# Summing an attention unit's values over all chunks of keys in one open PSUM bank

## The chip, the cores and the metric

The kernel runs on one core of a Trainium2 chip. The core has TensorE (PE, with its weight loads shown as PEld), VectorE (DVE), ScalarE (ACT), GpSimd (POOL) and SyncE (SP), which here only issues DMAs. TensorE writes its results to PSUM; the kernel plans with eight banks of 512 fp32 columns by 128 partitions. The metric is the device time of one execution in microseconds.

## The reference

Two layers (L0, L1) work on x of 4 x 512 x 320. Each layer has self-attention, cross-attention to a context of 4 x 1601 x 192, and a gated feed-forward part, all with a layer norm ahead and a residual behind. There are 20 heads of 16.

```python
def _attn(x, ctx, wq, wk, wv, wo, bo, heads):
    q = (x @ wq).reshape(b, n, heads, dh).transpose(0, 2, 1, 3)
    k = (ctx @ wk).reshape(b, j, heads, dh).transpose(0, 2, 1, 3)
    v = (ctx @ wv).reshape(b, j, heads, dh).transpose(0, 2, 1, 3)
    sim = jnp.einsum('bhid,bhjd->bhij', q, k) * scale
    a = jax.nn.softmax(sim, axis=-1)
    out = jnp.einsum('bhij,bhjd->bhid', a, v)
    return out.transpose(0, 2, 1, 3).reshape(b, n, heads * dh) @ wo + bo

h1 = _ln(x, n1_g, n1_b);  x = _attn(h1, h1, q1, k1, v1, o1_w, o1_b, heads) + x
h2 = _ln(x, n2_g, n2_b);  x = _attn(h2, context, q2, k2, v2, o2_w, o2_b, heads) + x
h3 = _ln(x, n3_g, n3_b)
a, g = jnp.split(h3 @ ff_w1 + ff_b1, 2, axis=-1)
x = a * jax.nn.gelu(g, approximate=False) @ ff_w2 + ff_b2 + x
```

## The kernel before

**Units and chunks.** The work is cut into units: one kind of attention, one batch element, one group of four heads. A layer has 20 self units and 20 cross units, then four feed-forward units. An attention unit goes over its keys in chunks of 128: 4 chunks in a self unit (512 keys), 13 in a cross unit (1601 keys, the last chunk has 65). The four heads of a group lie on four blocks of 32 partitions, so that four matmuls of 32 rows can run beside each other.

**One chunk.** `main` (L1272) does for each chunk two rounds, one for heads 0 and 1 and one for heads 2 and 3. A round takes two score tiles `st` (128 keys x 512 queries, three matmuls each: two with the split queries, L1285, and one that subtracts the maximum, L1288) and, beside them, usually two tiles `sps` of the *next* unit (L1093), from which VectorE finds that unit's maxima over the keys (L1112; a rest tile in L1131). ScalarE takes the exponential of each `st` into a buffer in SBUF (L1298); `place()` (L249) hands out these buffers in a ring of 9 or 12. `round_of` (L1258) interleaves the matmuls of scores and maxima, so that one kind runs on partitions 0 to 63 while the other runs on 64 to 127; in the second round the scores of heads 2 and 3 begin before the maxima tiles. If the unit in hand is ahead of schedule with maxima, extra rounds of them alone are put in.

**The values.** `values(c)` (L1305) multiplies the exponentials of chunk c with the values: four heads fill the four blocks of 32 partitions of one bank `av` (eight matmul instructions in the trace, L1312). It is held back by one chunk (`late`, `flush`): it is issued behind the scores of chunk c+1, and the last chunk's values behind the first scores of the next unit. Each chunk's `av` is a result of its own. ScalarE copies the first into `u.o` (L1323); each later one goes by a ScalarE copy into a ring buffer (L1328) and a GpSimd addition onto `u.o` (L1329). In the last cross unit of a layer, marked `last`, VectorE copies and adds instead (L1323, L1325), and no maxima run beside the scores. After the last chunk `add_finish` (L1168) puts the store of `u.o`, and after a batch element's fifth group the division by the sums and the output projection (`ops`, L1225), on the list of other work.

**Other work and its order.** Projections of queries (`qps`, L876), keys (`kps`, L910 for self and L953 for the context, the latter four banks at a time, read by ScalarE and VectorE in L963) and values (`vps`, L1028, and L1046 for the context, four banks at a time, read in L1054), norms, transposes and output projections wait in queues with costs and due times. `steps` (L471) takes from them behind each chunk's values, by rounds and credits. The order of PE's instructions comes from these rounds and credits.

**Banks.** Which of the eight banks a tile gets is planned in Python when the program is written out. `Pace` (L54) books an estimated time for every matmul, exponential, copy and maximum; `bank` (L161) takes the bank with the earliest booked release (`first`, L66), and marks it as taken (`give`, L71) until an instruction of ScalarE or VectorE that reads it is booked (`see`, L81). On the chip the first matmul into a bank waits for the last reader of the bank's previous tile. PE has one queue: what stands behind a waiting matmul waits with it.

Of the kernel before, what the change touches and what calls it, by code (L numbers as in the profile page):

```python
# [13 lines left out]
ALU = mybir.AluOpType  # L14
# [39 lines left out]
class Pace:  # L54
# [16 lines left out]
    def give(self, i, t):  # L71
        self.bank_of = {n: k for n, k in self.bank_of.items() if k != i}
        self.bank_of[t.tensor.name] = i
        self.opens[i] = self.free[i]
        self.free[i] = 1e9
# [5 lines left out]
    def see(self, r):  # L81
        i = r.ins
        kind = type(i).__name__
        banks = {self.bank_of.get(x.bass_ap.tensor.name) for x in list(i.ins) + list(i.outs) if hasattr(x, "bass_ap")}
        banks.discard(None)
        sizes = []
        for x in list(i.outs) + list(i.ins):
            if hasattr(x, "bass_ap"):
                n = 1
                for _, k in list(x.ap)[1:]:  # L90
                    n *= k
                sizes.append(n)
        if kind == "InstMatmult":
            (b,) = banks
            mode = tuple(i.tile_size or (P, P))
            if mode != self.mode:
                self.at["PE"] = max([self.at["PE"], *self.tiles.values()]) + 0.25
                self.tiles, self.mode = {}, mode
            pos = tuple(i.tile_position or (0, 0))
            self.at["PE"] = max(self.at["PE"], self.opens.get(b, 0.0) + 0.1)  # L100
            one = i.ins[0].dtype == F32R
            cost = max(sizes[0] * (1 if one else 4) / 2280, 0.06)
            self.tiles[pos] = max(self.tiles.get(pos, 0.0), self.at["PE"]) + cost
            self.ready[b] = self.tiles[pos]
            return r
        eng = "ACT" if "Activat" in str(i.engine) else "DVE"
        n = max(sizes)
        cost, more, late = (0.112 + n / 1400, 0.16, 0.1) if eng == "ACT" else (0.065 + n / 960, 0.16, 0.17)
        if eng == "DVE" and not banks:
            cost = 0.13 + n / 5900 if "Transpose" in kind else 0.18 + n / 960  # L110
        start = max([self.at[eng]] + [self.ready[b] + late for b in banks])
        self.at[eng] = start + cost
        for b in banks:
            self.free[b] = start + cost + more
        return r
# [13 lines left out]
def kernel(ctx: ExitStack, tc: tile.TileContext, x, context, ws, out):  # L129
# [18 lines left out]
    nc = tc.nc  # L148
# [8 lines left out]
    ps = ctx.enter_context(tc.tile_pool(name="ps", bufs=1, space=PSUM))  # L157
    pace_of = Pace()
    see = pace_of.see

    def bank(name, shape=(P, 512)):  # L161
        i = pace_of.first()
        t = ps.tile(list(shape), F32, tag=f"bank{i}", name=name)
        pace_of.give(i, t)
        return t
# [83 lines left out]
    def place():  # L249
        these = places[at_place["kind"]]  # L250
        at_place["i"] = (at_place["i"] + 1) % len(these)
        return these[at_place["i"]]
# [158 lines left out]
    start = {"on": True}  # L411
# [31 lines left out]
    def run(chain):  # L443
        costs, _, ready, _, f = chains[chain].popleft()
        assert ready(), chain
        f()
        clock["credit"] -= sum(costs)
# [15 lines left out]
    def next_cost():  # L463
        name = pick()
        return None if name is None else sum(chains[name][0][0])

    def tick():
        clock["round"] += 1
        clock["credit"] = max(-2.0, min(4.0, clock["credit"] + pace()))
# [34 lines left out]
    def until(test, name):  # L504
        while not test():
            assert chains[name], name
            run(name)
# [638 lines left out]
    def max_reduce(u):  # L1146
        if u.pm is not None:
            see(nc.vector.tensor_reduce(
                u.nm.rearrange("p (j t) -> p t j", t=NQ), u.pm, AX.X, ALU.max, negate=True
            ))  # L1150
# [102 lines left out]
    def flush():  # L1253
        for f in late:
            f()
        late.clear()

    def round_of(scores, maxima, turn=False):  # L1258

        todo = [f() for f in scores] + [f() for f in maxima]  # L1260
        if len(todo) == 3 and turn and [len(p) for p, _ in todo] == [3, 3, 2]:
            for j, i in [(0, 0), (1, 0), (0, 1), (1, 1), (2, 0), (2, 1), (0, 2), (1, 2)]:
                todo[j][0][i]()
        else:
            for i in range(max((len(passes) for passes, _ in todo), default=0)):
                for passes, _ in todo:
                    if i < len(passes):
                        passes[i]()
        for _, then in todo:
            then()  # L1270

    def main(u, give, nxt):  # L1272

        pr = {}
        if at_place["kind"] != u.kind:
            at_place.update(kind=u.kind, i=min(at_place["i"], len(mine) - 1))

        def score(c, j):
            r = min(P, u.nkeys - c * P)
            rows = slice(j * SLOT, (j + 1) * SLOT)  # L1280
            st = bank("st")
            keys = u.kT[rows, u.k0 + u.cols[c] : u.k0 + u.cols[c] + r].bitcast(F32R)

            def product(e):
                see(nc.tensor.matmul(st[:r, :], lhsT=keys, rhs=u.q[rows, :, e].bitcast(F32R), start=(e == 0), stop=False))  # L1285

            def less_maximum():
                see(nc.tensor.matmul(  # L1288
                    st[:r, :],
                    lhsT=units_of[rows, :r].bitcast(F32R),  # L1290
                    rhs=u.mrow[rows, :].bitcast(F32R),
                    start=False,
                    stop=True,
                ))

            def exponential():
                p = place()
                see(nc.scalar.activation(p[:r], st[:r], AF.Exp))  # L1298
                pr[c, j] = p

            return [lambda: product(0), lambda: product(1), less_maximum], exponential

        last = nxt is None or nxt.kind == "ff"

        def values(c):  # L1305
            if u.g in (0, 2):
                until(lambda: units[u.i - u.g].vmade[u.g // 2] > c, "values")
            ps = bank("av")
            r = min(P, u.nkeys - c * P)
            for j in range(HG):  # L1310
                head = (c * H + u.g * HG + j) * VW
                see(nc.tensor.matmul(  # L1312
                    ps[j * SLOT : (j + 1) * SLOT, :],
                    lhsT=columns_of[:r, head : head + SLOT],
                    rhs=pr.pop((c, j))[:r, :],
                    start=True,
                    stop=True,
                ))
            u.valued = c + 1

            if c == 0:
                u.o = three.tile([P, N], F32, tag="o", name="o")
                see((nc.vector.tensor_copy if last else nc.scalar.copy)(u.o, ps))  # L1323
            elif last:
                see(nc.vector.tensor_tensor(u.o, ps, u.o, ALU.add))  # L1325
            else:
                vo = place()
                see(nc.scalar.copy(vo, ps))  # L1328
                nc.gpsimd.tensor_tensor(u.o, u.o, vo, ALU.add)  # L1329
            if u.valued == u.nch:  # L1330
                add_finish(u)

        for c in range(u.nch):
            extra = []
            if last:

                round_of([lambda j=j: score(c, j) for j in range(HG)], [])
                tick()
            else:
                for odd in range(2):  # L1340
                    if odd:
                        tick()
                    pair, rounds = give(2 * c + odd)
                    extra += rounds
                    round_of([lambda j=j: score(c, j) for j in ((2, 3) if odd else (0, 1))], pair, odd)
            u.scored = c + 1

            if extra:
                round_of([], extra[0])
            flush()  # L1350
            late.append(lambda c=c: values(c))
            steps(None, 1 if extra or c == u.nch - 1 else 3)
            for i, e in enumerate(extra[1:]):
                if i and next_cost() is not None:
                    run(pick())
                round_of([], e)
            if not last and c == u.nch - 3:
                max_reduce(nxt)
                max_end(nxt)
            if loads:  # L1360
                loads.popleft()()
# [300 lines left out]
```

## Time and profile before

| | |
|---|---|
| median of 3 runs | 2959.55 us (2958.13 to 2960.76) |
| profiled execution, first to last instruction | 2956.1 us |
| around it, to the median | 3.5 us |
| granted TensorE clock, mean | 0.998 |
| PE busy | 2905.4 us (98%) |
| VectorE busy | 2017.1 us (68%) |
| ScalarE busy | 1950.7 us (66%) |
| GpSimd busy | 1361.8 us (46%) |

The first layer's self-attention runs to about 370 us, its cross-attention to about 1190, its feed-forward part to about 1500; the second layer follows in the same order. In a row of a group, `av<-pr,vals` names the tile written and the tiles read, then come partitions and elements, the count, the busy time, the mean duration in ns of one, and the idle time before them with what ended it. Buffers of the ring carry several names (`pr`, `wself`, `w`, `w1r`), since the ring borrows room in weight tiles. In a row of waits stand the engine that waited, what it waited for, the total in us, how many times, and the longest. In a timeline stand the start and the duration in us, the engine, the line and what it does; a bracket gives the idle time of the engine before it and what ended that. A busy PE in this profile is not PE at its peak: matmuls overlap, and their ends are modelled.

### The profile page before, as it was taken

Reading aid. Unit: us, or ns where it says so; the run is one execution under the profiler, and the core shown is the slowest. Engines: PE = TensorE matmul, PEld = TensorE weight load, DVE = VectorE, ACT = ScalarE, POOL = GpSimd, SP = SyncE. Lnnn points to the kernel's source line nnn. Section 1 sums busy time; section 2 is a strip of 40 time slices with the busy share of each in tenths; the row PEclk is TensorE's granted clock in tenths of the full one; section 3 lists DMA queues with packets and bytes.
Section 4 is the critical chain, followed back from the end, with each engine's and each line's share of the span. In section 5 each row is a group of like instructions: output and inputs, shape, how many; then the busy total and the mean of one; then the engine's idle time right before and its main releaser. Section 6 shows DMA issues by size and latency. Waiting matters only on the chain.

```text
span 2956.1 us, 92200 instructions
## 1 busy us (share of the span) xinstructions
PE 2905.4 (98%) x37842; PEld 1608.3 (54%) x37842; DVE 2017.1 (68%) x3893; ACT 1950.7 (66%) x4029; POOL 1361.8 (46%) x1714
## 2 busy tenths in 40 slices
PE   9999999999999999999999999999999999999999
PEld 4555556555555555455554555655555555544555
DVE  7777887887888788322257778878878878872221
ACT  4867677887887888511147766778878888893111
POOL 4556455555555554312125664555555555541110
PEclk9999999999999999999999999999999999999999
DMA  4434222222122221300124332121221221212000
GB/s 117 120 102 116 68 71 55 55 71 70 32 71 64 48 56 28 113 6 0 33 53 112 95 95 74 50 69 34 60 70 36 58 69 43 52 52 57 12 11 12
DMA packets 221151, 178.01 MB, mean 60 GB/s; under 512 B 137652, under 2 KB 175416, under 8 KB 220728
## 3 DMA queue, kind: packets, MB, share of 16 engines
q1 hardware_dynamic: 219928, 171.05, 22.4%
q8 instruction: 297, 4.87, 0.7%
q10 hardware_dynamic: 800, 1.06, 0.1%
q14 instruction: 126, 1.03, 0.1%
HBM read 54.67 MB, written 29.56 MB: 28 GB/s over the span
## 4 chain that ended last, share of the span: by engine, by line
PE 88%; DVE 7%; ACT 2%; POOL 1%; issue 1%; DMA 1%; SPq 0%; ACTq 0%; POOLq 0%; DVEq 0%
PE av L1312 22%; PE st L1285 15%; PE sps L1093 11%; PE fps L1407 9%; PE yps L1462 6%; PE kps L953 4%; PE ops L1225 4%; DVE pm L1112 3%; PE st L1288 3%; PE qps L876 3%; PE vps L1046 3%; PE fps L1420 2%; DVE nmax L1112 2%; PE vps L1028 2%; PE kps L910 2%
## 5 line engine op out<-in xcount | busy, mean ns | idle before, releaser
L1112 DVE TENSOR_REDUCE pm<-sps 128x1 f32<-128x512 f32 x1920 | 1190.4, 681 | 100.3 <-PE sps L1093 93.8
L1093 PE MATMUL sps<-kT,q 32*128 32x512 f32 (+1 forms) x6400 | 1059.6, 401 | 10.3 <-DMA kT<-stage 3.5
L1298 ACT ACTIVATE pr<-st 128x512 f32<-128x512 f32 (+1 forms) x1710 | 905.0, 603 | 182.1 <-PE st L1288 170.3
L1285 PE MATMUL st<-q,kT 32*128 32x512 f32 (+1 forms) x5440 | 864.4, 423 | 2.1 <-ACT stage L918 1.2
L1329 POOL TENSOR_TENSOR o<-o,pr 128x512 f32<-128x512 f32 x359 | 460.2, 1282 | 583.0 <-ACT pr L1328 575.4
L1312 PE MATMUL av<-pr,vals 128*32 128x512 f32 (+1 forms) x3420 | 632.8, 605 | 21.0 <-DVE nmax L1112 2.8
L1285 PEld LDWEIGHTS st<-q,kT 32*128 32x128 f32 (+1 forms) x5440 | 461.9, 180 | 351.0 <-ACT pr L1298 133.8
L1093 PEld LDWEIGHTS sps<-kT,q 32*128 32x128 f32 x6400 | 554.8, 183 | 96.0 <-ACT pr L1298 11.6
L1288 PE MATMUL st<-m,units 32*128 32x512 f32 (+1 forms) x2720 | 550.5, 399 | 1.0 <-DMA m<-turned 0.9
L1298 ACT ACTIVATE wself<-st 128x512 f32<-128x512 f32 (+1 forms) x867 | 463.2, 604 | 79.7 <-PE st L1288 74.9
L1112 DVE TENSOR_REDUCE nmax<-sps 128x1 f32<-128x512 f32 x640 | 397.2, 682 | 112.6 <-PE sps L1093 111.1
L1329 POOL TENSOR_TENSOR o<-o,wself 128x512 f32<-128x512 f32 x191 | 244.8, 1282 | 287.9 <-ACT wself L1328 277.9
L1312 PE MATMUL av<-wself,vals 128*32 128x512 f32 (+1 forms) x1734 | 368.6, 605 | 8.1 <-ACT pr L1298 1.6
L1407 PE MATMUL fps<-hT,w 128*128 128x512 f32 x640 | 283.7, 596 | 0.0
L1430 ACT ACTIVATE pr<-fps,b 128x512 f32<-128x512 f32 x80 | 54.7, 687 | 346.0 <-PE fps L1420 245.4
L1288 PEld LDWEIGHTS st<-m,units 32*128 32x128 f32 (+1 forms) x2720 | 251.6, 180 | 20.0 <-POOL stage L765 1.1
L1328 ACT COPY pr<-av 128x512 f32<-128x512 f32 x359 | 220.6, 615 | 11.6 <-PE av L1312 11.2
L1407 PEld LDWEIGHTS fps<-hT,w 128*128 128x128 f32 x640 | 118.8, 190 | 149.4 <-issue 148.5
L1312 PEld LDWEIGHTS av<-pr,vals 128*32 128x32 f32 (+1 forms) x3420 | 91.2, 108 | 187.8 <-DVE pm L1112 83.3
L765 POOL TENSOR_SCALAR stage<-stage 128x256 fp32r<-128x256 f32 (+1 forms) x155 | 106.2, 685 | 158.6 <-ACT stage L918 82.9
L953 PEld LDWEIGHTS kps<-ctxT,w 32*128 32x128 f32 (+1 forms) x4992 | 112.6, 160 | 40.7 <-ACT pr L1298 17.8
L1225 PEld LDWEIGHTS ops<-wo,aT 112*32 112x32 f32 (+1 forms) x3072 | 98.6, 110 | 64.4 <-issue 39.6
(115 smaller groups left out, 3068.1 us busy)
## 6 DMA issues: line engine op xcount, KB each, us to landing
q<-stage SPq DMA_DIRECT2D x154, 256.0 KB
kT<-w SPq DMA_DIRECT2D x120, 208.0 KB
outs<-o SPq DMA_DIRECT2D x80, 256.0 KB
kT<-stage SPq DMA_DIRECT2D x76, 128.0 KB
aT<-outs SPq DMA_DIRECT2D x32, 224.0 KB
oturn<-over SPq DMA_DIRECT2D x32, 224.0 KB
kT<-w SPq DMA_DIRECT2D x40, 144.0 KB
w<-in_L_xattn_ff_w_dram SPq DMA_DIRECT2D x20, 256.0 KB
```

The costliest lines, as they stand in the source:

```text
L953: see(nc.tensor.matmul(ps[to : to + n, :PIECE], lhsT=wk_q[rows, k, u.g * GD : u.g * GD + n], rhs=first.kvT[rows, k, at : at + PIECE], star ...
L1093: see(nc.tensor.matmul(out, lhsT=u.q[rows, t // 2, e, t % 2 * P : (t % 2 + 1) * P].bitcast(F32R), rhs=u.kT[rows, keys].bitcast(F32R), star ...
L1112: see(nc.vector.tensor_reduce(to[:, j : j + 1], ps, AX.X, ALU.max, negate=(ns == 1)))
L1225: see(nc.tensor.matmul(ps[f : f + m, : D // 2], lhsT=aT[:n, k, t * P + f : t * P + f + m], rhs=wo[:n, k, cols], start=(k == 0), stop=(k == 2),
L1285: see(nc.tensor.matmul(st[:r, :], lhsT=keys, rhs=u.q[rows, :, e].bitcast(F32R), start=(e == 0), stop=False))
L1288: see(nc.tensor.matmul(st[:r, :], lhsT=units_of[rows, :r].bitcast(F32R), rhs=u.mrow[rows, :].bitcast(F32R), start=False, stop=True,))
L1298: see(nc.scalar.activation(p[:r], st[:r], AF.Exp))
L1312: see(nc.tensor.matmul(ps[j * SLOT : (j + 1) * SLOT, :], lhsT=columns_of[:r, head : head + SLOT], rhs=pr.pop((c, j))[:r, :], start=True, s ...
L1328: see(nc.scalar.copy(vo, ps))
L1329: nc.gpsimd.tensor_tensor(u.o, u.o, vo, ALU.add)
L1407: see(nc.tensor.matmul(ps, lhsT=w1[:, k, i * FF + c * P : i * FF + (c + 1) * P], rhs=u.hT[:, k, :], start=ahead and k == 0, stop=not ahead ...
L1462: see(nc.tensor.matmul(ps[:, :D], lhsT=hid[c][:, t * P : (t + 1) * P], rhs=w2[:, c, :], start=(c == 0), stop=(c == NHC - 1),))
```

## The change

A unit takes one bank for `av` when its first values are computed and keeps it until its last. The first chunk's matmuls start the sum, the others add to it, and one copy takes it to `u.o` after the last chunk (by ScalarE, in a `last` unit by VectorE). The copies and additions of the other chunks go: 3 of each in a self unit, 12 in a cross unit. The matmuls, their order and the due times stay.

```diff
         def values(c):
             if u.g in (0, 2):
                 until(lambda: units[u.i - u.g].vmade[u.g // 2] > c, "values")
-            ps = bank("av")
+            if c == 0:
+                u.av = bank("av")
+            ps = u.av
             r = min(P, u.nkeys - c * P)
             for j in range(HG):
                 head = (c * H + u.g * HG + j) * VW
...
                     rhs=pr.pop((c, j))[:r, :],
-                    start=True,
-                    stop=True,
+                    start=(c == 0),
+                    stop=(c == u.nch - 1),
                 ))
             u.valued = c + 1
 
-            if c == 0:
+            if u.valued == u.nch:
                 u.o = three.tile([P, N], F32, tag="o", name="o")
                 see((nc.vector.tensor_copy if last else nc.scalar.copy)(u.o, ps))
-            elif last:
-                see(nc.vector.tensor_tensor(u.o, ps, u.o, ALU.add))
-            else:
-                vo = place()
-                see(nc.scalar.copy(vo, ps))
-                nc.gpsimd.tensor_tensor(u.o, u.o, vo, ALU.add)
-            if u.valued == u.nch:
                 add_finish(u)
```

## The prediction

> **What bounds the kernel now.** I read the page's head and its chain of waits first, then the list of waits, then the timeline of a few chunks. The page:
>
> ```profile
> span 2956.1 us, 92200 instructions
> ...
> PE 2905.4 (98%) x37842; PEld 1608.3 (54%) x37842; DVE 2017.1 (68%) x3893; ACT 1950.7 (66%) x4029; POOL 1361.8 (46%) x1714
> ...
> PE 88%; DVE 7%; ACT 2%; POOL 1%; issue 1%; DMA 1%; SPq 0%; ACTq 0%; POOLq 0%; DVEq 0%
> ...
> L1298 ACT ACTIVATE pr<-st 128x512 f32<-128x512 f32 (+1 forms) x1710 | 905.0, 603 | 182.1 <-PE st L1288 170.3
> L1329 POOL TENSOR_TENSOR o<-o,pr 128x512 f32<-128x512 f32 x359 | 460.2, 1282 | 583.0 <-ACT pr L1328 575.4
> L1312 PE MATMUL av<-pr,vals 128*32 128x512 f32 (+1 forms) x3420 | 632.8, 605 | 21.0 <-DVE nmax L1112 2.8
> ...
> L1328 ACT COPY pr<-av 128x512 f32<-128x512 f32 x359 | 220.6, 615 | 11.6 <-PE av L1312 11.2
> ```
>
> TensorE is busy 98% of the span and carries 88% of the chain; ScalarE and GpSimd, from which the change takes work, carry 3% together. So what the change does to the time is decided by what it does to PE, and PE keeps every one of its matmuls. What can move is only when a PSUM bank is free for the next matmul. The list of waits says which banks PE's weight loads wait for:
>
> ```profile
> PEld av L1312 <- DVE pm L1112: 141.5, 328, 0.8
> ...
> PEld st L1285 <- ACT pr L1298: 133.8, 208, 0.8
> ...
> PEld av L1312 <- DVE nmax L1112: 59.0, 117, 1.4
> ...
> PEld av L1312 <- ACT pr L1298: 42.3, 98, 0.7
> ...
> PEld sps L1093 <- ACT pr L1298: 11.6, 33, 0.8
> ...
> PEld sps L1093 <- ACT pr L1328: 8.8, 54, 0.3
> ...
> PEld sps L1093 <- ACT wself L1328: 5.6, 35, 0.3
> ```
>
> The totals hold PE's change from one tile shape to the next, so they are no stalls by themselves. What counts is the names. The bank for `av` is most often one that VectorE has just released by a maximum (328 and 117 times), and 54 + 35 times a maximum tile `sps` waited for the copy out of `av`, which the change removes. The kernel runs at the edge of its eight banks. Two chunks of a cross-attention unit show how:
>
> ```profile
> 651.50 0.50 PE L1285 MATMUL st<-q,kT 32*128 32x512 f32 x2
> ...
> 651.51 0.65 PE L1093 MATMUL sps<-kT,q 32*128 32x512 f32 x2
> ...
> 651.96 0.62 ACT L1328 COPY wself<-av 128x512 f32<-128x512 f32 x1
> ...
> 652.31 0.48 PE L1093 MATMUL sps<-kT,q 32*128 32x512 f32 x1
> ...
> 652.63 0.18 PEld L1093 LDWEIGHTS sps<-kT,q 32*128 32x128 f32 x2 [0.16 <-ACT wself L1328]
> ...
> 653.29 1.07 PE L1312 MATMUL av<-pr,vals 128*32 128x512 f32 x8
> ...
> 654.28 0.50 PE L1285 MATMUL st<-q,kT 32*128 32x512 f32 x2
> ...
> 654.29 0.50 PE L1093 MATMUL sps<-kT,q 32*128 32x512 f32 x2
> ...
> 655.07 2.48 DVE L1112 TENSOR_REDUCE pm<-sps 128x1 f32<-128x512 f32 x4 [0.29 <-PE sps L1093]
> ...
> 655.16 0.54 PE L1093 MATMUL sps<-kT,q 32*128 32x512 f32 x2
> ...
> 655.34 2.06 ACT L1298 ACTIVATE pr<-st 128x512 f32<-128x512 f32 x4 [0.23 <-PE st L1288]
> ...
> 655.82 0.16 PEld L1312 LDWEIGHTS av<-wself,vals 128*32 128x32 f32 x8 [0.36 <-DVE pm L1112]
> 655.82 1.06 PE L1312 MATMUL av<-wself,vals 128*32 128x512 f32 x8
> ```
>
> The groups of maxima, by count, shortest/median/longest in ns, and first and last start:
>
> ```profile
> L1112 DVE TENSOR_REDUCE pm<-sps x1920: 623/681/694, 277.1 to 2637.7; 128x1 f32<-128x512 f32 x192
> L1112 DVE TENSOR_REDUCE nmax<-sps x640: 648/681/694, 20.0 to 1811.8; 128x1 f32<-128x512 f32 x160
> L1131 DVE TENSOR_REDUCE pm<-sps x160: 421/424/438, 362.0 to 2640.6; 128x4 f32<-128x264 f32 x160
> ```
>
> A chunk opens eight tiles in PSUM: two `st` and two `sps` at its start (654.28), two more `st` half a microsecond on, and the last `sps` (call it the eighth tile) at 655.16. The first of the eight to be released is a maximum: VectorE starts it at 655.07, it takes 0.68 (681 ns, below), so its bank is free at 655.75. At 655.16 all eight are therefore unread, and all eight banks are taken. `av` is the ninth tile: it starts at 655.82, when the first maximum ends. In the chunk at 651.50 the eighth tile had to wait instead until the copy out of the previous `av` (651.96 + 0.62) was done, and began at 652.63. So `av` borrows the eighth bank for a part of each chunk only.
>
> **The change part by part.**
>
> *The bank that stays open.* After the change `av` holds a bank from a unit's first values to its last, and seven are left for the eight tiles of a chunk. The order of PE's matmuls does not depend on the banks (they are laid out by rounds and credits), so the eighth tile must wait, in its old place, for a tile of its own chunk. In the second chunk that is the release that `av` waits for now: 655.82 instead of 655.16, 0.66 us late. PE's later matmuls stand behind it in order. From the eighth tile to `av` it is 0.66 us in both chunks (652.63 to 653.29, 655.16 to 655.82), and then `av` itself has nothing left to wait for; so `av` moves from 655.82 to 656.48 and the chunk grows by 0.66. In the first chunk the same release would come 1.54 after its start (655.82 - 654.28), at 653.04; the eighth tile now starts at 652.63, so it loses 0.41. The copy's lateness that this chunk pays today is thereby already given back.
>
> I take the two as equally frequent: the waits of `sps` for the copy are 89 of 680 chunks, but `st` and `sps` wait some 240 times more for exponentials of the chunk before (rows above), which makes the eighth tile late in the same way. Mean 0.535 us. Chunks: 40 self units of 4 and 40 cross units of 13 are 680. In the second chunk of each unit no values bank is open while the scores run (80 chunks), and the last cross unit of each layer has no maxima beside its scores (26, of which 2 are second chunks). That leaves 680 - 80 - 24 = 576, and 576 x 0.535 = **+308 us**. Lower end: 0.41 everywhere, +236. Upper end: the planner gives the eighth tile the bank of an `st`; the first exponential of the second chunk starts at 655.34 and takes 0.60 (603 ns in the page's row of L1298), so the release is at 655.94, 0.19 later: 576 x 0.725 = +418.
>
> *Chunks behind a group of four tiles.* The projections of keys and values from the context open four banks at once, and scores often follow at once:
>
> ```profile
> 805.69 2.23 PE L1046 MATMUL vps<-w,ctxT 32*128 32x192 f32 x48
> ...
> 807.61 0.54 PE L1285 MATMUL st<-q,kT 32*65 32x512 f32 x2
> ...
> 807.94 0.54 ACT L1054 COPY vals<-vps 128x192 f32<-128x192 f32 x2 [1.35 <-PE vps L1046]
> ...
> 807.98 0.62 DVE L1054 COPY vals<-vps 128x192 f32<-128x192 f32 x2 [1.51 <-PE vps L1046]
> ...
> 808.31 0.27 PEld L1285 LDWEIGHTS st<-q,kT 32*65 32x65 f32 x4 [0.19 <-ACT vals L1054]
> ```
>
> ```profile
> L1054 ACT COPY vals<-vps x96: 265/296/328, 324.4 to 2494.8; 128x128 f32<-128x128 f32 x48, 128x192 f32<-128x192 f32 x48
> ```
>
> ```profile
> L963 ACT COPY w<-kps x160: 245/248/254, 239.2 to 2577.9; 128x104 f32<-128x104 f32 x160
> ```
>
> At 807.61 four banks hold `vps`, four are free. With `av` open there are three, so the fourth tile waits for the first copy: 807.94 + 0.30 = 808.24, 0.63 late, and the wait for the eighth tile comes on top. There are 96/2 = 48 such groups of values and 160/2 = 80 of keys (half of each group's four copies are ScalarE's). Ends: nothing (hidden by another step in between) and 128 x 0.63 = +81. I take three quarters of the groups at 0.5 us, since the copies of `kps` are shorter: 96 x 0.5 = **+48 us**.
>
> *The copies and sums that go.* 40 x 3 + 40 x 12 less the 24 of the `last` units, again 576, chunks lose a ScalarE copy of 615 ns (354 us of ScalarE) and a GpSimd addition of 1282 ns (738 us); in the `last` unit of each layer 24 additions of VectorE go. On the path this is worth only the lateness counted above, since none of these engines carries the chain; PE's 98% of busy time is what hides it. If PE had slack, ScalarE would give at most its 2% of the chain, 59 us. ScalarE's queue gains: exponentials no longer stand behind a copy, but the first exponential of a chunk already waits for PE (655.34 above). GpSimd's other work moves forward, which nothing on the chain waits for. The ring of buffers for the probabilities loses one of five users per chunk, so its reuse comes later, worth 0.
>
> *Accumulating in PSUM.* The same matmuls run with another start flag.
>
> ```profile
> L1285 PE MATMUL st<-q,kT 32*128 32x512 f32 (+1 forms) x5440 | 864.4, 423 | 2.1 <-ACT stage L918 1.2
> ...
> L1288 PE MATMUL st<-m,units 32*128 32x512 f32 (+1 forms) x2720 | 550.5, 399 | 1.0 <-DMA m<-turned 0.9
> ```
>
> L1288 only adds to a started bank, half of L1285 starts one, and the adding line is not the longer: 0. The store of a unit's output is issued three rounds after the last values in both kernels, on the same queue; 0.
>
> *Two rules of the Trainium skill.* The row to set beside them is the wait of `av` for the first maximum at 655.82. "Perfetto Trace Analysis", section "Optimization Strategy", says that the same gap repeating on the engine that should be saturated can mean that there is not enough PSUM for the next tile. By it the change buys ScalarE and GpSimd time, which is not short, with a bank, which is. The trace agrees, and the sum by this rule is the one below. "PSUM — Partial Sum Buffer", section "Summary: rules for kernel authors", says to evacuate PSUM promptly; the present kernel does, the changed one doesn't. [...]
>
> **Sum.** The span of the profiled execution is 2956.1, 3.5 us under the median of the runs, 2959.55. Against the span: 2956.1 + 308 + 48 = 3312; with the 3.5 around it 3315.5. I say **3315 us**.
>
> **Rivals.**
>
> *The change gains.* If the eighth tile never had to wait for its own chunk, the late copies would go: 0.41 is 0.25 less than 0.66, so each late chunk holds 0.25 us, and the rows name 54 + 35 of them; with the some 240 others that is at most 330 x 0.25 = 82, at the named ones 22. Middle about 42: 2917 us. It decides where the first release of a chunk lies: 0.88 after its start (655.16 - 654.28) or earlier, instead of 1.47. VectorE's start 0.79 after the chunk's plus 0.68 speaks against it, and I see no way round it. Chance 5%.
>
> *Many chunks do not open eight tiles.* If half of them opened fewer maxima beside their scores, half the sum: 2959 + 178 = 3137. For it: maxima are also given ahead in extra rounds. Against: 1920 + 640 maxima and 160 of the rest tile are 2720, four for each of 680 chunks. With it I count the case that VectorE, 68% busy, catches up in the longer chunks and releases earlier. Chance 8%.
>
> *The waits chain.* If the planner, which books a time for each release, puts a tile of a chunk's first half into the bank that is released last, each chunk pays a second wait. By the rows: exponentials run 655.34 to 657.40, and the next chunk would start at 656.48 + 0.99 = 657.47, so the last release is just in time. A misplaced bank costs perhaps 0.35: 576 x 0.35 = 202 more, 3517 us. Chance 8%.
>
> **How the numbers follow.** Forecast 79%, with 3200 to 3420 as its own range: 2959.55 + 236 = 3196 without the groups of four, 2959.55 + 418 + 48 = 3426 with the exponentials' release. The three rivals have 5, 8 and 8. The range 3190 to 3430 holds the forecast's case and leaves the rivals out. Faster by over 0.2% (about what a measurement of this kernel can tell from no change) is the first rival, 5%; within 0.2% I give 1%; slower 94%.
>
> **What would show it.** In the profile after: the lines of copies and additions shrink to 80 copies, ScalarE loses about 350 us, GpSimd about 740. PE's matmuls keep their counts and mean durations, and the waits for banks move from `av` to `sps` L1093: several hundred waits for L1112 or L1298, where the rows above name 33 for an exponential. `av` no longer waits for VectorE except in 80 places. The eighth tile of a chunk starts about 1.5 us after the chunk, not 0.9, and `av` 2.2 after, not 1.5 to 1.8. The FFN stretches keep their lengths. The prediction is wrong if `sps` starts on time while `av` is open, or if the waits lie at the start of a chunk instead of at its eighth tile.

## The result, and the profile after

The changed kernel takes 3306.15 us (median of 4 runs, 3301.82 to 3306.55) where the kernel before takes 2960.16. The ratio is 1.1169, 95% interval 1.1153 to 1.1185: slower by 346 us, 9 us less than predicted.

The page of the changed kernel, its busy times, its chain and the groups that answer to those shown before:

```profile
span 3304.6 us, 90182 instructions
...
PE 3105.8 (94%) x37842; PEld 1618.5 (49%) x37842; DVE 2054.4 (62%) x3869; ACT 1741.1 (53%) x3453; POOL 632.0 (19%) x1138
...
PE 81%; DVE 13%; issue 3%; ACT 2%; POOL 0%; DMA 0%; SPq 0%; ACTq 0%; DVEq 0%; POOLq 0%
...
L1093 PE MATMUL sps<-kT,q 32*128 32x512 f32 (+1 forms) x6400 | 1234.7, 410 | 180.7 <-DVE pm L1112 110.6
...
L1298 ACT ACTIVATE pr<-st 128x512 f32<-128x512 f32 (+1 forms) x1710 | 935.3, 597 | 462.1 <-PE st L1288 370.7
```

PE has the same 37842 matmuls. GpSimd has lost more than half of its work, ScalarE 210 us, and the kernel is slower: VectorE's share of the chain has gone from 7% to 13%, although VectorE executes 24 instructions fewer (3869, not 3893; its busy time is 37 us longer). PE now sits idle in front of the maximum tiles `sps`: the row of L1093 above has 180.7 us of idle time, and on the page of the kernel before it had 10.3:

```profile
L1093 PE MATMUL sps<-kT,q 32*128 32x512 f32 (+1 forms) x6400 | 1059.6, 401 | 10.3 <-DMA kT<-stage 3.5
```

The list of waits of the changed kernel says for what:

```profile
PEld sps L1093 <- DVE pm L1112: 278.4, 391, 0.9
...
PEld av L1314 <- issue: 206.4, 564, 0.4
...
PE sps L1093 <- DVE pm L1112: 110.6, 320, 0.5
...
PEld sps L1093 <- DVE nmax L1112: 65.8, 94, 1.2
...
PEld sps L1093 <- ACT pr L1298: 39.7, 63, 1.9
```

The rows have changed places. Before, `av` waited for VectorE's maxima and `sps` hardly ever did; now `sps` waits 391 + 94 times for a maximum. Of the weight loads of `av`, 564 are listed as waiting for nothing (`issue`); further down the list, 30 + 32 still wait for a maximum (30 us in all), all of them in the second chunk of a unit, where no bank is open yet. The two chunks that the prediction walked through lie at 730.48 and 733.66 in the new timeline:

```profile
730.48 0.49 PE L1285 MATMUL st<-q,kT 32*128 32x512 f32 x2
...
730.48 0.50 PE L1093 MATMUL sps<-kT,q 32*128 32x512 f32 x2
...
731.26 2.58 DVE L1112 TENSOR_REDUCE pm<-sps 128x1 f32<-128x512 f32 x4 [0.61 <-PE sps L1093]
...
732.00 0.51 PE L1093 MATMUL sps<-kT,q 32*128 32x512 f32 x2 [0.33 <-DVE pm L1112]
...
732.66 0.11 PEld L1314 LDWEIGHTS av<-pr,vals 128*32 128x32 f32 x2 [0.37 <-issue]
...
733.66 0.49 PE L1285 MATMUL st<-q,kT 32*128 32x512 f32 x2
...
734.44 2.57 DVE L1112 TENSOR_REDUCE pm<-sps 128x1 f32<-128x512 f32 x4 [0.60 <-PE sps L1093]
...
735.18 0.49 PE L1093 MATMUL sps<-kT,q 32*128 32x512 f32 x2 [0.33 <-DVE pm L1112]
...
735.84 0.12 PEld L1314 LDWEIGHTS av<-wself,vals 128*32 128x32 f32 x3 [0.36 <-issue]
```

In both, the eighth tile starts 1.52 us after the chunk (732.00 - 730.48, 735.18 - 733.66), just behind the first maximum (731.26 + 0.68 = 731.94), and `av` follows 0.66 later. The first chunk used to have its `av` 1.79 after its start and the second 1.54; now both have it at 2.18.

Matching the 680 chunks of the two traces one by one, from a chunk's first score matmul to the values that are issued behind its scores, gives the whole account:

| chunks | number | longer by, mean | sum |
|---|---|---|---|
| bank open, eight tiles | 499 | 0.536 us | +267 us |
| the same, behind a group of four tiles | 77 | 0.980 us | +75 us |
| second chunk of a unit (no bank open) | 78 | -0.135 us | -11 us |
| last unit of a layer (no maxima) | 26 | 0.005 us | 0 |
| all time outside these stretches | | | +16 us |

That is 348 us, the difference of the spans (3304.6 - 2956.1). Two of the 499 are the first chunk of a layer, where no bank is open and which have no values behind their scores (they are taken to the next chunk's values); the other 497 have a mean of 0.541. The two kinds that the prediction took from the timeline are there, but not in equal numbers: 222 of the 497 lie within 0.05 us of 0.66, 99 within 0.05 of 0.41, and the rest between them or outside.

A chunk behind a group of four, the one shown before at 807.61:

```profile
913.58 0.53 PE L1285 MATMUL st<-q,kT 32*65 32x512 f32 x2
...
913.91 0.54 ACT L1054 COPY vals<-vps 128x192 f32<-128x192 f32 x2 [1.96 <-PE vps L1046]
...
914.28 0.18 PEld L1093 LDWEIGHTS sps<-kT,q 32*128 32x128 f32 x1 [0.53 <-ACT vals L1054]
...
915.79 0.50 PE L1093 MATMUL sps<-kT,q 32*128 32x512 f32 x2 [0.31 <-ACT pr L1298]
```

The fourth tile waits for the first copy out of `vps` (914.28, 0.70 after the chunk's start), and the eighth again, at 915.79, for an exponential.

The feed-forward part of the second layer has kept its length and its work: from the first to the last matmul of its two products it takes 274.7 us in both traces (2678.0 to 2952.7, 3026.5 to 3301.2). Two windows of the same length over it hold nearly the same work. They are in us from the start; behind the length stand the busy times of PE, PEld, VectorE, ScalarE and GpSimd, the clock, the DMA share and GB/s. First the kernel before, then the changed one:

```profile
2674.00:2956.00 282.00, 278.69 (x1056) 145.21 (x1052) 58.32 (x110) 38.16 (x57) 27.92 (x81) 1.00 0.05 16
```

```profile
3022.00:3304.00 282.00, 279.25 (x1061) 145.35 (x1056) 56.92 (x108) 38.74 (x58) 27.93 (x81) 1.00 0.05 16
```

### The profile page after: what moved, and what is told of

It is laid out like the page before. It is cut to its first block, busy times and chain, and to the rows that moved or that the text cites. A ratio compares the mean times of both kernels' runs of the same rounds, so it can differ in the third digit from the quotient of the medians.

```text
span 3304.6 us, 90182 instructions
## 1 busy us (share of the span) xinstructions
PE 3105.8 (94%) x37842; PEld 1618.5 (49%) x37842; DVE 2054.4 (62%) x3869; ACT 1741.1 (53%) x3453; POOL 632.0 (19%) x1138
## 4 chain that ended last, share of the span: by engine, by line
PE 81%; DVE 13%; issue 3%; ACT 2%; POOL 0%; DMA 0%; SPq 0%; ACTq 0%; DVEq 0%; POOLq 0%
PE av L1314 20%; PE sps L1093 17%; PE st L1285 12%; DVE pm L1112 9%; PE fps L1402 8%; PE yps L1457 5%; PE ops L1225 3%; PE qps L876 3%; DVE nmax L1112 3%; PE vps L1046 3%; PE fps L1415 2%; PE vps L1028 2%; PE kps L953 2%; PE kps L910 1%; PE st L1288 1%
## 5 line engine op out<-in xcount | busy, mean ns | idle before, releaser
L1093 PE MATMUL sps<-kT,q 32*128 32x512 f32 (+1 forms) x6400 | 1234.7, 410 | 180.7 <-DVE pm L1112 110.6
L1112 DVE TENSOR_REDUCE pm<-sps 128x1 f32<-128x512 f32 x1920 | 1226.1, 684 | 249.7 <-PE sps L1093 236.6
L1298 ACT ACTIVATE pr<-st 128x512 f32<-128x512 f32 (+1 forms) x1710 | 935.3, 597 | 462.1 <-PE st L1288 370.7
L1093 PEld LDWEIGHTS sps<-kT,q 32*128 32x128 f32 x6400 | 576.0, 183 | 475.8 <-DVE pm L1112 278.4
L1314 PE MATMUL av<-pr,vals 128*32 128x512 f32 (+1 forms) x3420 | 725.2, 608 | 3.1 <-ACT pr L1298 0.4
L1298 ACT ACTIVATE wself<-st 128x512 f32<-128x512 f32 (+1 forms) x870 | 478.6, 597 | 205.0 <-PE st L1288 142.3
L1288 PE MATMUL st<-m,units 32*128 32x512 f32 (+1 forms) x2720 | 581.8, 430 | 0.7 <-DMA m<-turned 0.6
L765 POOL TENSOR_SCALAR w<-w 128x416 fp32r<-128x416 f32 x80 | 100.2, 1252 | 870.7 <-DVE w L963 448.5
L953 PE MATMUL kps<-ctxT,w 32*128 32x104 f32 (+1 forms) x4992 | 130.7, 269 | 4.7 <-ACT w L963 3.0
L1225 PE MATMUL ops<-wo,aT 112*32 112x160 f32 (+1 forms) x3072 | 124.9, 299 | 0.0
```

What stands on the lines that cost most here:

```text
L765: eng.tensor_scalar(high.bitcast(F32R), x, 1.0, None, ALU.mult)
L953: see(nc.tensor.matmul(ps[to : to + n, :PIECE], lhsT=wk_q[rows, k, u.g * GD : u.g * GD + n], rhs=first.kvT[rows, k, at : at + PIECE], star ...
L1093: see(nc.tensor.matmul(out, lhsT=u.q[rows, t // 2, e, t % 2 * P : (t % 2 + 1) * P].bitcast(F32R), rhs=u.kT[rows, keys].bitcast(F32R), star ...
L1112: see(nc.vector.tensor_reduce(to[:, j : j + 1], ps, AX.X, ALU.max, negate=(ns == 1)))
L1225: see(nc.tensor.matmul(ps[f : f + m, : D // 2], lhsT=aT[:n, k, t * P + f : t * P + f + m], rhs=wo[:n, k, cols], start=(k == 0), stop=(k == 2),
L1288: see(nc.tensor.matmul(st[:r, :], lhsT=units_of[rows, :r].bitcast(F32R), rhs=u.mrow[rows, :].bitcast(F32R), start=False, stop=True,))
```

## The experiments

The theory: all that is lost is a bank. Rivals: that accumulating in one bank, or the later copy, costs PE time of its own; that the removed copies and additions had been worth more, or nothing.

**One bank fewer, nothing else.** The kernel before, with its copies and additions, on seven banks:

```diff
+        self.banks = 8
...
-        i = min(range(8), key=lambda i: self.free[i])
+        i = min(range(self.banks), key=lambda i: self.free[i])
...
+        pace_of.banks = 8 if u.kind == "ff" else 7
         (ff_main if u.kind == "ff" else main)(u, giver(u), nxt)
```

> The kernel before with its copies and additions, but the planner may use only seven banks in the attention units (eight in the feed-forward units, which need them at once). No bank stays open, nothing accumulates over chunks. Theory (a bank is all that is lost): the eighth tile waits for a release of its own chunk as in the changed kernel, and it does so in the second chunk of a unit as well: 3306 + 80 x 0.535 = 3349, between 3290 and 3420. Rival (the open bank's accumulation or the order of the reads costs the time): 2960 to 3050.

Measured: 3359.06 us against 2958.87, ratio 1.1353 (1.132 to 1.1385). The kernel has no open bank and accumulates nothing across chunks, and it loses 400 us. Its waits of `sps` are those of the changed kernel; `av`, which here needs a bank in every chunk, waits for an exponential:

```profile
PEld sps L1094 <- DVE pm L1113: 255.2, 426, 0.8
...
PEld av L1313 <- ACT pr L1299: 128.7, 352, 0.5
...
PE sps L1094 <- DVE pm L1113: 96.7, 350, 0.5
...
PEld sps L1094 <- DVE nmax L1113: 91.1, 135, 1.4
```

These waits of `av` add nothing: in both kernels it starts 0.31 us, in the mean, behind the last matmul of a score or maximum tile. Matched with the kernel before, the 499 chunks are longer by 0.549 us each; the changed kernel has 0.536. The second chunks of the units, which the change spares, here pay 0.560 each (44 us), which is most of the difference between 3359 and 3306. The rival that PE pays for accumulating has fallen: as large a loss comes without any.

**Another bank fewer.** The changed kernel with the same edit, so that six are left beside the open one.

```diff
+        self.banks = 8
...
-        i = min(range(8), key=lambda i: self.free[i])
+        i = min(range(self.banks), key=lambda i: self.free[i])
...
+        pace_of.banks = 8 if u.kind == "ff" else 7
         (ff_main if u.kind == "ff" else main)(u, giver(u), nxt)
```

> The changed kernel with seven banks in the attention units, so that six are left beside the open one. Theory: now the seventh tile of a chunk waits for the first release (about 1.5 us after the chunk's start) and the eighth for the second: an exponential's, 0.17 later, or the second maximum's, 0.68 later. 3306 + 576 x 0.17 = 3404 to 3306 + 576 x 0.68 = 3698; middle 3550. Rival (PE's loss is not a matter of banks): 3306.

Measured: 3469.85 us, ratio 1.1727 (1.1693 to 1.1761) to the kernel before. This is the chunk that was at 730.48:

```profile
774.59 0.49 PE L1286 MATMUL st<-q,kT 32*128 32x512 f32 x2
...
775.37 1.29 DVE L1113 TENSOR_REDUCE pm<-sps 128x1 f32<-128x512 f32 x2 [0.57 <-PE sps L1094]
775.64 1.09 ACT L1299 ACTIVATE wself<-st 128x512 f32<-128x512 f32 x2 [0.77 <-PE st L1289]
776.11 0.37 PEld L1094 LDWEIGHTS sps<-kT,q 32*128 32x128 f32 x3 [0.76 <-DVE pm L1113]
...
776.95 0.11 PEld L1315 LDWEIGHTS av<-pr,vals 128*32 128x32 f32 x2 [0.37 <-issue]
```

Now the seventh tile waits for the first maximum (776.11, 1.52 after the start), and `av` comes 2.36 after the start (776.95 - 774.59), 0.18 later than in the changed kernel. The eighth tile goes to the bank of the first exponential: in the trace its first matmul starts at 776.29, just behind the end of that exponential (776.24), while the second maximum ends only at 776.66. 499 chunks at 0.184 are 92 us of the 164 between the two kernels. The second chunks of the units pay 56 us more, which the expectation had forgotten: with one more bank gone they lose their eighth too. The groups of four pay 20. The time lies inside the expected range, 80 us under its middle, because most chunks go by the nearer of the two releases that were expected.

**One tile fewer.** Head 1 takes the maxima of head 0; VectorE reads head 0's tile twice, so its work stays. The edit goes into the changed kernel and, as a control, into the kernel before.

```diff
-            pss = [bank("sps") for _ in heads]
+            pss = [bank("sps") for _ in heads[: 1 + heads[0] // 2]]
+            pss = (pss * 2)[:2]
...
-            return passes(heads, pss, t, keys), reduce
+            return passes(heads[: 1 + heads[0] // 2], pss, t, keys), reduce
```

(The rest tile is edited in the same way.)

> The changed kernel, with one maximum tile fewer per chunk: head 1 takes the maxima of head 0, whose tile VectorE reads twice, so VectorE's work stays, and a chunk opens seven tiles beside the open bank. Left out: the scores of head 1 for its own maxima. Theory (the loss is the wait for an eighth bank): the wait goes, and the time is that of the same edit made to the kernel before, within 2%: about 2890, between 2840 and 2960; the waits of sps for VectorE drop from several hundred to under 150. Rival (accumulating in one bank, or the later copy, costs PE time): it stays about 350 us above the same edit of the kernel before, 3200 or more.

> The kernel before with the same edit: head 1 takes the maxima of head 0, seven tiles per chunk. It is the control for the changed kernel with seven tiles. Theory: there are now eight banks for seven tiles and av, so the late eighth tiles (22 to 82 us) and the wait of av for the first maximum (0.07 us in some 500 chunks, 35 us) go: 2850 to 2910. Rival (banks do not bind the kernel before at all): 2950 to 2963.

Measured: the changed kernel with seven tiles takes 2921.26 us, the control 2876.64; ratios to the kernel before 0.9872 (0.9857 to 0.9886) and 0.972 (0.9703 to 0.9736). One tile fewer is worth 385 us to the changed kernel and 83 us to the kernel before. The edit also takes 1600 of PE's 37842 matmuls away, from both kernels alike, so it is the difference of the two, 302 us, that speaks of the bank. The waits of `sps` in the changed kernel with seven tiles:

```profile
PEld sps L1093 <- ACT vals L1054: 16.2, 34, 0.5
PEld sps L1093 <- DVE pm L1113: 11.8, 33, 0.6
...
PEld sps L1093 <- ACT w L963: 10.4, 26, 0.7
```

391 waits for a maximum `pm` have become 33, and the 94 for `nmax` have become 9. What is left names the groups of four, `vals` and `w`, and there lies most of the 45 us between the two: matched chunk by chunk, the 77 chunks behind such a group are longer by 0.37 us each (28 us), the 499 others by 0.016 in the mean (8 us). In those 499, PE accumulates in one bank as in the changed kernel, and they cost nearly nothing more. So the groups of four pay with seven banks even where the eighth tile is gone, as the prediction's second term had it.

The control is the fastest kernel of the study, but no replacement for the one before: a maximum that belongs to another head doesn't bound the exponentials for every input.

**The removed work alone.** Each chunk's values keep a bank of their own, which counts as free at once; the copies and additions are left out, and with them the sums over the chunks.

```diff
-            if c == 0:
+            if u.valued == u.nch:
                 u.o = three.tile([P, N], F32, tag="o", name="o")
                 see((nc.vector.tensor_copy if last else nc.scalar.copy)(u.o, ps))
...
+                add_finish(u)
+            else:
+                pace_of.unread(ps)
```

> The kernel before, with each chunk's values in a bank of their own as it was, but no copies and no additions except for a unit's last chunk; the bank counts as free when its matmuls end. The sums over the chunks are left out, so the outputs are not those of the reference. This is the removed work alone, without the open bank. Theory (the copies cost only the lateness of the eighth tile, 22 to 82 us; nothing else is on the path): about 2917 us, between 2875 and 2940, ScalarE busy about 1600 and GpSimd about 630. Rival (ScalarE's and GpSimd's work matters in its own right, and the change lost far more than it shows): 2600 to 2800. Rival (the copies were wholly hidden): 2955 to 2963.

Measured: 2923.99 us, ratio 0.988 (0.9865 to 0.9895). The whole of ScalarE's copies and GpSimd's additions was worth 35 us where nothing is paid for it.

```profile
PE 2870.7 (98%) x37842; PEld 1603.1 (55%) x37842; DVE 1999.4 (68%) x3869; ACT 1682.7 (58%) x3453; POOL 633.8 (22%) x1138
```

PE is again busy 98% of the span, though ScalarE and GpSimd have shrunk as in the changed kernel. ScalarE's 1682.7 us are more than the 1600 or so that were expected. Nearly all of the 35 us lies between a chunk's first scores and the values behind them: the 499 chunks lose 0.069 each, together 34, of which 4.5 fall in the very first chunk. The loss is uneven (a quarter of them 0.08 or more, a twentieth 0.26), as late eighth tiles would have it; that each of these is a late eighth tile is not shown.

**Pairs of chunks.** The bank is opened in an even chunk and closed, copied and added in the next.

```diff
-            ps = bank("av")
+            if c % 2 == 0:
+                u.av = bank("av")
+            ps = u.av
+            ends = c % 2 == 1 or c == u.nch - 1
...
-                    start=True,
-                    stop=True,
+                    start=(c % 2 == 0),
+                    stop=ends,
...
-            if c == 0:
+            if not ends:
+                return
+            if c == 1:
```

> The change done over two chunks at a time: av is opened in an even chunk and closed, copied and added in the next. The bank is open during the scores of 6 of 13 chunks in a cross unit and 2 of 4 in a self unit, 308 chunks after the two last units are taken off, where the change has 576. Theory (each chunk with the bank open pays 0.535 us and its share of the groups of four): 2960 + 346 x 308/576 = 3145, between 3090 and 3190. Rival (the loss comes with the first accumulation, whatever its length): near 3306. Rival (the loss comes from the one copy at the unit's end): near 2960.

Measured: 3116.91 us, ratio 1.0531 (1.051 to 1.0552), 158 us where 185 was expected. The 282 chunks whose scores run with the bank open, with eight tiles and no group of four ahead, pay 0.537 each, 151 us; the 26 with the bank open behind a group of four pay 24. The 344 others that have maxima beside their scores are shorter by 0.05 each, 18 us together, which the expectation had put at 0. The loss follows the number of chunks whose scores run with the bank open, not the number of accumulations and not the copy at the end.

## Why the prediction was right

**The open bank (308 us).** Right in its mechanism and its place. The eighth tile waits for the first maximum of its own chunk, `av` follows 0.66 us later, and the chunks that pay are the 576 that were counted, but for the first of each layer. The mean of 0.536 over 499 of them, against 0.535, is in part luck: equal weights for the two kinds were a choice without a row of its own, and the kinds are not equal (222 chunks near 0.66, 99 near 0.41); chunks between the two and below them bring the mean back. The upper end, an exponential's release for the eighth tile, was not what most chunks do (63 waits of `sps` for `pr` of L1298 against 485 for a maximum), but with one bank fewer it happened, at 0.184 where 0.19 was estimated.

**Groups of four (48 us).** The mechanism is right, the size 34: 0.44 more than the others each (0.980 - 0.536), not 0.5, in 77 chunks. Directly ahead of a chunk there are just 96 groups, the number that was guessed as three quarters of 128, but 19 of them stand ahead of a unit's second chunk, where no bank is open.

**The copies and sums that go.** 35 us where nothing else changes, inside the 22 to 82 that the first rival was priced with. In the changed kernel only the second chunks of the units could still show some of it, and they are 11 us shorter; the prediction had put them at 0. Against that stand 16 us outside the stretches from scores to values, which no step had and whose cause stays open. The sum came out 9 us high; that it came so close is in part luck, since 14 us too many for the groups and the 11 us here are made up for by these 16.

**Accumulating at no cost.** Shown by the kernel on seven banks, which pays as much without it, and by the 0.016 us that the 499 chunks with seven tiles are longer in the mean.

**What would show it.** The waits moved as said, the eighth tile is at 1.52 and `av` at 2.18, the feed-forward part kept its length. ScalarE was to lose about 350 us and lost 210. Count times mean is too much, since a copy of 615 ns overlaps its neighbours in the busy time: where only the copies are left out, 268 us go (1950.7 to 1682.7). And in the changed kernel the exponentials stand in pairs (one row of two at 731.53 in the trace, where a row at 655.34 had four), overlap less, and cover more (905 us before, 935 after, for one of their groups).

**The rivals.** A gain did not come, and the point from which it would have come was well placed: the first release stands 1.46 after the chunk's start (731.94 - 730.48), not at 0.88 or earlier, and only where a tile is taken away does the changed kernel beat the one before. That many chunks open fewer than eight tiles has fallen: the 576 chunks pay the full mean. Chained waits did not show: the 499 chunks are longer by a single wait.

## What to carry to other kernels

Before a result is left standing in a PSUM bank, count the tiles that are unread at once in one turn of the loop, and look up in a timeline when the first of them is released: if they fill the banks, the bank is paid for on TensorE, as it was here, by the distance from the last tile's matmul to that release, in every turn. Work taken off engines that carry 3% of the chain returned 35 us here where nothing was paid for it; with the bank that it took, the change lost 346. Where a wait moves from one tile to another, what matters is how much of the same engine's work stands behind its new place (here 0.66 us, from the eighth tile to `av`).

## What the runs showed of the hardware that was not expected

In the kernel before, whose PE is busy for 98% of the span, one tile fewer per chunk still gave 83 us (2876.64), more than twice what the copies' removal gave. Matched chunk by chunk, 48 us of it lie between the last matmul of a score or maximum tile and `av` (0.38 us before in the mean, 0.32 with one tile fewer): `av`, the ninth tile, had itself been waiting for a release. The other 35 lie ahead of that matmul, where the late eighth tiles are, and also the 1600 matmuls that the edit takes away; the two are not told apart. PE's busy row shows only a part of this as idle time: the time outside it goes from 50.7 us (2956.1 - 2905.4) to 23.9 (2876.2 - 2852.3), 27 of the 80 us between the two spans. The Trainium skill's "Perfetto Trace Analysis", section "Matmul Optimizations", says to make use of all eight PSUM banks; here the eighth is worth 400 us (3359.06 against 2958.87).
